# A graph layer on one core: gathers planned with a longer landing and seven tiles kept, first ranks with 128 columns of weights, evictions planned 0.3 later

## The chip, the cores and the metric

The kernel runs on one core of one Trainium2 chip. The metric is the device time of one execution, in microseconds. Before the change the median of three runs is 625.49 us (624.39 to 628.74).

## What is computed

There are 6250 nodes with 128 features each, and 100,000 edges of two types, sorted by their destination. Every edge sends its source's features through the matrix of its type; each node adds up what arrives, adds its own product with a third matrix, and the result goes through a relu, a residual sum and a layer normalisation.

```python
Xs = X[src]
m_data = Xs @ W_data.T + b_data
m_ctrl = Xs @ W_control.T + b_control
msg = jnp.where((edge_types == 0)[:, None], m_data, m_ctrl)
agg = jax.ops.segment_sum(msg, dst, num_segments=X.shape[0])
out = jax.nn.relu(agg + (X @ W_self.T + b_self))
x = _layernorm(x + out)
```

## The kernel before, in words

The nodes are 49 blocks of 128. In the start, `multiply` (L458) forms both products of every block in PSUM (`y`, float32, 128 columns of weights at a time), and `take`, `leave` and `last_part` split each into three bfloat16 parts of 128 columns, together 384: ScalarE copies a part, TensorE subtracts it in PSUM with the matrix `minus` (L483, L496), and so on. The parts stay in SBUF as `m3` and are stored by SP to `table` in DRAM in seven portions of 4, 8, 8, 8, 8, 8 and 5 blocks, two DMAs each (`store`, L509).

35 blocks (`GROUPS`, seven groups of five) sort their edges on the chip. For each group `bucket_hots` (L567) marks edges by source block and type, and `ranks` (L571) gives every edge a place within its bucket: per step of 18, a matmul with `tri` into `acc`, a maximum on VectorE (L584), and a matmul with `rest` into the same `acc`. `fill_a` and `fill_b` (L621, 98 columns, ten matmuls per step `v`) bring the source numbers to their places, ScalarE copies the result (`vs`, L634), and `fill_c` sends it to DRAM (`packed`, L639). `spread` (L739) reads it back, spread over all partitions, as `rows`; `select` (L746) compares it with the partition's number. The main stage then works tile by tile, 25 tiles to a block: `gather` (L775) picks rows of `m3` by matmuls with `rows` as weights into `g_ps` (four banks, `GB`), `evict` (L790) casts them to `gs` (eight tiles, `EB`), mostly on ScalarE, and in the last group partly on VectorE, and `add_up` sums them per destination in `agg` by matmuls with `hot_d`. Nearly all these matmuls have 32 columns of weights and come in fours, one for each strip of the array: `by_columns` (L228, L231) does this.

The other 14 blocks are gathered in another way: `gather_rows` (L877) has GpSimd fetch the rows of 128 edges at a time from `table` by an indirect DMA into `msg` (252 of them, `MB` tiles), once all of `table` is stored, and `gathered_sums` sums them in `agg_g` with `hot_g`. The few edges for which a bucket has no place are fetched on the same GpSimd queue (L715, `mixed`). A finished block goes through `add_parts` (L153), `finish`, `stats`, and by group through `normalise` (L189 on ScalarE) to the output.

The order of instructions on each engine is written by a planner, `Order` (L59). Each part of the work is a stream of steps; a step has a name, a cost for each engine that may take it, names of steps that it needs, and a `lag` between its end on the engine and the time at which others may count on it. The planner holds a time per engine, adds 0.25 between a step and one that needs it, and takes among the steps that could begin next the one that is due first (`due`, L389). Its times only decide the order (and, where two engines may take a step, which one does); on the chip the engines wait for semaphores. A tile's bank or buffer comes free by the same means: gather i needs eviction i - 4, message i needs the gathered sum i - 5.

Of the kernel before, what the change touches and what calls it, by code (L numbers as in the profile page):

```python
# [19 lines left out]
P = 128  # L20
# [7 lines left out]
KT = 18  # L28
# [25 lines left out]
KC = 6  # L54
# [46 lines left out]
def step(name, costs, *needs, lag=0.0):  # L101
    return as_tuple(name), costs, [as_tuple(n) for n in needs], lag


def as_tuple(name):
    return name if isinstance(name, tuple) else (name,)
# [3 lines left out]
def kernel(  # L110
# [94 lines left out]
    with ExitStack() as main:  # L205
        sums_over_windows(main, tc, x, xt, edges, w, bias, table, packed, total,
                          add_parts, finish, load_rows, norm)
# [6 lines left out]
def sums_over_windows(ctx, tc, x, xt, edges, w, bias, table, packed, total,  # L214
                      add_parts, finish, load_rows, norm):
    nc = tc.nc
    V, A, G, T = nc.vector, nc.scalar, nc.gpsimd, nc.tensor
# [7 lines left out]
    order = Order()  # L225
    YB = 4

    def by_columns(out, lhsT, rhs, **flags):  # L228

        for c in range(0, P, 32):  # L230
            T.matmul(out[c : c + 32], lhsT[:, c : c + 32], rhs, **flags)  # L231


    r0 = const.tile([EC, RJ], I32, name="r0")
# [49 lines left out]
    for j in range(RJ):  # L284
# [7 lines left out]
        out=er.rearrange("p k c -> p (k c)"), out_offset=None,  # L292
# [11 lines left out]
    tri = const.tile([P, P], BF16, name="tri")  # L304
    rest = const.tile([P, P], BF16, name="rest")
# [80 lines left out]
    PACE = 1.68  # L386
# [184 lines left out]
    def ranks():  # L571
        for grp, n in enumerate(GROUPS):
            free = [("rank", grp - 1, KT - 1)] if grp else []
            for k in range(KT):
                yield step(("tri", grp, k), {"T": 0.21}, ("hot", grp, k // KC), *free)
                if k == 0:
                    acc = ps_a.tile([P, 512], F32, name="acc")
                    flat = acc[:, : n * NT]
                    by_q = flat.rearrange("p (s q) -> p q s", q=n)
                hot = hots[grp, k // KC][:, k % KC].rearrange("p s q -> p (s q)")  # L580
                by_columns(flat, tri, hot, start=k == 0, stop=False, skip_group_check=True)
                free = []
                yield step(("rank", grp, k), {"V": 0.13 + 0.103 * n}, ("tri", grp, k))
                V.tensor_reduce(slots[grp][:, k, :], by_q, axis=AX.X, op=ALU.max)  # L584
                if k == KT - 1:
                    break
                yield step(("rest", grp, k), {"T": 0.21}, ("rank", grp, k))
                by_columns(flat, rest, hot, start=False, stop=k == KT - 2, skip_group_check=True)

    def fill_a():  # L590
        for grp, n in enumerate(GROUPS):
# [16 lines left out]
    def fill_b():  # L608
        for grp, n in enumerate(GROUPS):
            free = [("listed", grp - 1)] if grp else ["first"]  # L610
            for k in range(KT):
                yield step(("v", grp, k), {"T": 0.07 * n}, ("two", grp, k // KC), *free)
                if k == 0:
                    vts[grp] = ps_a.tile([P, 512], F32, name="small")
                vt = vts[grp][:, : (n + 1) // 2 * NT].rearrange("p (j s) -> p j s", s=NT)
                two = two_s[grp, k // KC]
                hot = hots[grp, k // KC]
                for q in range(n):
                    for i in range(2):
                        c0 = (q % 2 * 2 + i) * R  # L620
                        T.matmul(vt[c0 : c0 + R, q // 2, :], two[:, k % KC, i, :, q],  # L621
                                 hot[:, k % KC, :, q], start=k == 0 and q < 2,
                                 stop=k == KT - 1, skip_group_check=True)
                free = []
# [153 lines left out]
    def evict():  # L778
        for i, (b, g) in enumerate(tiles):
            free = [("s", *tiles[i - EB])] if i >= EB else []  # L780
            if g == NS - 1 and b:
                free.append(("s", b - 1, g))
            costs = {"A": 0.37, "V": 0.53} if b >= STARTS[-1] else {"A": 0.37}
            e = yield step(("e", b, g), costs, ("g", b, g), *free)
            if g < NS - 1:
                gs, at = late.tile([P, D3], BF16, name="gs", bufs=EB), slice(P)
            else:
                gs, at = mixed[blocks[b][0] % 2], slice(2 * R, P)
            gs_tiles[b, g] = gs
            (A.copy if e == "A" else V.tensor_copy)(gs[at], g_tiles.pop((b, g))[at, :D3])  # L790

    def add_up():
        for b, g in tiles:
            grp, q = blocks[b]
            free = [("agg", b)] if g == 0 else [("spilled", grp), ("o", b)] if g == NS - 1 else []
            yield step(("s", b, g), {"T": 0.165}, ("e", b, g), ("d", b, g // DC), *free)
            if g == 0:
                aggs[b] = ps_a.tile([P, D3], F32, name="agg")
            by_columns(aggs[b], d_hots[b, g // DC][:, :, g % DC], gs_tiles.pop((b, g)),
                       start=g == 0, stop=g == NS - 1, skip_group_check=True)  # L800
# [54 lines left out]
    rel_g = const.tile([P, NG, KT], BF16, name="rel_g")  # L855
    msgs, g_hots, kept = {}, {}, []
    GQ = -(-NG // -(-NG // Q))
    MB, XB = 5, 2

    def gathered_fields():  # L860
        yield step("idx", {"V": 1.8}, ("y", NB * 3 // 4), *[("win", b) for b in range(NPB, NB)])
# [10 lines left out]
    def gather_rows():  # L872
        for i, (j, k) in enumerate(gathered):
            free = [("gm", *gathered[i - MB])] if i >= MB else [*stored, "idx"]
            yield step(("msg", j, k), {"G": PACE}, *free, lag=3.0 - PACE)
            msgs[j, k] = late.tile([P, D3], BF16, name="msg", bufs=MB)
            G.indirect_dma_start(  # L877
                out=msgs[j, k], out_offset=None, in_=table[:, :],
                in_offset=bass.IndirectOffsetOnAxis(ap=idx[:, j, k : k + 1], axis=0),
            )  # L880
# [47 lines left out]
    def close_build():  # L928
# [5 lines left out]

    order.run([
        load_x(), starts(), edge_fields(), ranks(), fill_c(), fill_a(), fill_b(),
        spread(), select(), finish_blocks(),
        normalise([(lambda g=g: (hs_[g], mvs[g]), STARTS[g] + q0, q0, n) for g, q0, n in PIECES], "p"), add_up(), gather(), evict(), to_hots(), bucket_hots(),
        multiply(), take(0, "yh", "y"), leave(0, "y1", "yh"),
        take(1, "ym", "y1"), last_part(), constants(), store(), close_build(), add_counts(),  # L940
        finish_gathered(), gathered_sums(), gathered_hots(), gather_rows(), gathered_fields(),
        normalise([(lambda i=i: kept[i], NPB + i * GQ, 0, min(GQ, NG - i * GQ))
                   for i in range(-(-NG // GQ))], "g"),
# [129 lines left out]
```

## Time and profile before

| | |
|---|---|
| median of three runs | 625.49 us |
| the profiled execution's own time | 542.67 us |
| its span, first to last instruction | 540.9 us |
| mean granted TensorE clock | 0.984 |
| TensorE busy, weight loads busy | 507.3 us (94%), 442.9 us (82%) |
| VectorE, ScalarE, GpSimd busy | 432.4, 415.9, 297.4 us |
| L790, ScalarE cast of g_ps to gs | 807, mean 498 ns |
| L775, gather matmuls | 3430, mean 332 ns |
| L231, sums with hot_d, with hot_g | 3360 and 1008, mean 331 and 332 ns |
| L231, ranks with tri and rest | 504 and 476, mean 376 and 378 ns |
| L877, indirect DMAs of msg | 252, mean 1145 ns |

Matmuls on different strips of the array overlap, so the mean of one is not what it adds. SP's work is only issuing and waiting; its rows in a timeline are DMA issues. POOL is GpSimd, ACT ScalarE, DVE VectorE, PE TensorE and PEld its weight loads. A row of a timeline has the start and the duration in microseconds, and in brackets the idle time of the engine before it and what ended it. A row of waits has the total in microseconds, the number of times and the longest.

### The profile page before, as it was taken

To read this page: it belongs to the slowest core of one execution; us is meant where nothing else is said; L and a number is where in the kernel's file an instruction comes from. 1 tells how busy PE (TensorE), PEld (TensorE's weight loads), DVE (VectorE), ACT (ScalarE), POOL (GpSimd) and SP (SyncE) were. 2 spreads that over 40 slices of the span, in tenths; PEclk is the share of its full clock that TensorE was granted. 3 is DMA by queue.
4 is the path that set the end of the run, shared out by engine and by line. 5 is a ranking of instruction groups with operands and counts; after the bars stand their busy time and mean duration, and the time that the engine had idled before them with its cause. 6 is when DMAs were issued, how large, how long until landed. Compare 5 with 4: busy or idle time off the path is not lost.

```text
span 540.9 us, 26355 instructions
## 1 busy us (share of the span) xinstructions
PE 507.3 (94%) x11204; PEld 442.9 (82%) x11204; DVE 432.4 (80%) x967; ACT 415.9 (77%) x1003; POOL 297.4 (55%) x267
## 2 busy tenths in 40 slices
PE   5799977999999999999999999999999999999993
PEld 3546547799887998988989899999998999889882
DVE  5587889578987789978799878999789667668784
ACT  6654356577869788798888888877979879889793
POOL 1000002777687676776567676775757756677500
PEclk9999998799999999999999999999999999999998
DMA  3566875542555425554354542544445454555301
GB/s 94 145 179 191 260 239 193 153 131 79 184 159 161 138 77 179 157 169 134 99 194 139 164 139 81 183 139 160 142 134 162 133 156 135 180 166 164 115 17 35
DMA packets 60932, 79.19 MB, mean 146 GB/s; under 512 B 15760, under 2 KB 51371, under 8 KB 60807
## 3 DMA queue, kind: packets, MB, share of 16 engines
q1 hardware_dynamic: 47253, 49.14, 27.8%
q0 software_dynamic: 12400, 25.08, 16.9%
q10 hardware_dynamic: 1154, 3.21, 1.9%
q8 instruction: 89, 1.46, 1.1%
q14 instruction: 36, 0.29, 0.2%
HBM read 64.35 MB, written 13.05 MB: 143 GB/s over the span
## 4 chain that ended last, share of the span: by engine, by line
PE 73%; DMA 9%; ACT 5%; DVE 5%; issue 3%; SPq 3%; POOL 1%; ACTq 0%; DVEq 0%; POOLq 0%
PE agg L231 25%; PE g_ps L775 23%; PE acc L231 8%; PE agg_g L231 7%; PE small L621 6%; DMA msg<-table,idx 5%; ACT gs L790 2%; DMA rows<-packed 2%; PE y L465 2%; SPq L807 1%; POOL msg L877 1%; ACT h_p L189 1%; SPq L158 1%; DVE slot L584 1%; DVE hot_st L567 1%
## 5 line engine op out<-in xcount | busy, mean ns | idle before, releaser
L790 ACT CAST gs<-g_ps 128x384 bf16<-128x384 f32 x807 | 333.7, 498 | 72.4 <-PE g_ps L775 53.5
L877 POOL DMA_INDIRECT msg<-table,idx x252 | 288.5, 1145 | 115.4 <-PE g_ps L775 46.4
L775 PE MATMUL g_ps<-m,rows 128*32 128x384 bf16 x3430 | 322.4, 332 | 0.9 <-ACT gs L790 0.7
L231 PE MATMUL agg<-gs,hot_d 128*32 128x384 bf16 x3360 | 301.4, 331 | 3.3 <-ACT gs L790 3.3
L231 PEld LDWEIGHTS <-hot_d 128*32 128x32 bf16 x3500 | 195.8, 137 | 13.1 <-issue 7.1
L775 PEld LDWEIGHTS <-rows 128*32 128x32 bf16 x3430 | 189.8, 137 | 18.5 <-issue 12.7
L231 PE MATMUL agg_g<-msg,hot_g 128*32 128x384 bf16 x1008 | 109.1, 332 | 6.2 <-DMA msg<-table,idx 5.8
L584 DVE TENSOR_REDUCE slot<-acc 128x5 bf16<-128x490 f32 x126 | 83.6, 663 | 28.9 <-PE acc L231 17.7
L760 DVE TENSOR_TENSOR hot_d<-count,to 128x1664 bf16<-128x1664 bf16 x70 | 74.4, 1065 | 6.6 <-PE agg L231 6.0
L621 PE MATMUL small<-hot_st,two 128*32 128x98 bf16 x1260 | 70.2, 290 | 0.0
L231 PE MATMUL acc<-hot_st,tri 128*32 128x490 bf16 x504 | 61.8, 376 | 2.1 <-DVE hot_st L567 2.1
L231 PEld LDWEIGHTS <-hot_g 128*32 128x32 bf16 x1008 | 53.5, 123 | 10.6 <-issue 7.8
L231 PE MATMUL acc<-hot_st,rest 128*32 128x490 bf16 x476 | 56.8, 378 | 4.5 <-DVE slot L584 4.0
L621 PEld LDWEIGHTS <-two 128*32 128x32 bf16 x1260 | 58.3, 118 | 2.3 <-DVE two L605 0.6
L715 POOL DMA_INDIRECT mixed<-table,row_i x7 | 6.5, 933 | 92.9 <-DVE hot_g L889 82.3
L476 ACT CAST m<-y 128x512 bf16<-128x512 f32 (+1 forms) x50 | 28.1, 577 | 30.9 <-PE y L483 23.1
L567 DVE TENSOR_TENSOR hot_st<-count,st_b 128x2940 bf16<-128x2940 bf16 x21 | 41.8, 1996 | 7.6 <-PE small L621 5.3
L746 DVE TENSOR_SCALAR rows<-rows,pid 128x3136 bf16<-128x3136 bf16 x35 | 37.0, 1057 | 5.5 <-DMA rows<-packed 5.2
L153 DVE TENSOR_REDUCE whole<-agg 128x128 f32<-128x384 f32 x35 | 19.4, 553 | 17.6 <-PE agg L231 12.8
L465 PE MATMUL y<-w_sb,xt 128*128 128x256 f32 x98 | 33.2, 426 | 0.0
L231 PEld LDWEIGHTS <-rest 128*32 128x32 bf16 x476 | 22.1, 98 | 12.8 <-issue 11.8
L231 PEld LDWEIGHTS <-tri 128*32 128x32 bf16 x504 | 22.4, 99 | 3.3 <-issue 3.1
(144 smaller groups left out, 438.0 us busy)
## 6 DMA issues: line engine op xcount, KB each, us to landing
rows<-packed SPq DMA_DIRECT2D x35, 784.0 KB
table<-m SPq DMA_DIRECT2D x10, 768.0 KB
msg<-table,idx POOLq DMA_INDIRECT x252
xt<-in_xt ACTq DMA_DIRECT2D x5, 512.0 KB
xt_p<-in_xt SPq DMA_DIRECT2D x35, 64.0 KB
xs_p<-in_x SPq DMA_DIRECT2D x35, 64.0 KB
out<-h_p SPq DMA_DIRECT2D x6, 320.0 KB
table<-m SPq DMA_DIRECT2D x2, 480.0 KB
```

The lines of the kernel that those rows point to most:

```text
L153: nc.vector.tensor_reduce(whole, agg.rearrange("p (i c) -> p c i", i=3), axis=AX.X, op=ALU.add)
L231: T.matmul(out[c : c + 32], lhsT[:, c : c + 32], rhs, **flags)
L465: T.matmul(y[:, j, :], xts[g][:, b + j - at_part[g], :], w_sb[:, : 2 * D], start=j == 0, stop=False, skip_group_check=True)
L476: A.copy(part_of(b, n, i), ys[b][:, :n, :].rearrange("p b (t c) -> p t b c", t=2))
L567: V.tensor_tensor(hot, counted[n][:, None, 1 : NT + 1, :].to_broadcast([P, KC, NT, n]), fields[grp][2][:, c * KC : c * KC + KC, None, :].t ...
L584: V.tensor_reduce(slots[grp][:, k, :], by_q, axis=AX.X, op=ALU.max)
L621: T.matmul(vt[c0 : c0 + R, q // 2, :], two[:, k % KC, i, :, q], hot[:, k % KC, :, q], start=k == 0 and q < 2, stop=k == KT - 1, skip_group ...
L746: V.tensor_scalar(rows[b], rows[b], pid1, None, op0=ALU.is_equal)
L760: V.tensor_tensor(hot, counted[DC][:, :, :n], places[grp][:, q, None, c * DC : c * DC + n].to_broadcast([P, P, n]), op=ALU.is_equal)
L775: T.matmul(g_ps[t * R : (t + 1) * R, :D3], rows[b][:, :, s], m3[:, s, :], start=True, stop=True)
L790: (A.copy if e == "A" else V.tensor_copy)(gs[at], g_tiles.pop((b, g))[at, :D3])
L877: G.indirect_dma_start(out=msgs[j, k], out_offset=None, in_=table[:, :], in_offset=bass.IndirectOffsetOnAxis(ap=idx[:, j, k : k + 1], axis=0),
```

## The change

Four things change. `by_columns` gets a width, and the ranks of group 0 use 128: one matmul with 128 columns of weights in place of four with 32. In group 0 the steps `v` are planned six at a time, so that their matmuls follow each other. The lag of an eviction is 0.3 instead of 0. A message is planned with 4.2 instead of 3.0 from its issue to its landing, and seven tiles of `msg` are kept instead of five.

```diff
-    def by_columns(out, lhsT, rhs, **flags):
+    def by_columns(out, lhsT, rhs, width=32, **flags):
 
-        for c in range(0, P, 32):
-            T.matmul(out[c : c + 32], lhsT[:, c : c + 32], rhs, **flags)
+        for c in range(0, P, width):
+            T.matmul(out[c : c + width], lhsT[:, c : c + width], rhs, **flags)
...
     def ranks():
         for grp, n in enumerate(GROUPS):
             free = [("rank", grp - 1, KT - 1)] if grp else []
+            width = 32 if grp else P
...
-                by_columns(flat, tri, hot, start=k == 0, stop=False, skip_group_check=True)
+                by_columns(flat, tri, hot, width, start=k == 0, stop=False, skip_group_check=True)
...
-                by_columns(flat, rest, hot, start=False, stop=k == KT - 2, skip_group_check=True)
+                by_columns(flat, rest, hot, width, start=False, stop=k == KT - 2, skip_group_check=True)
...
-                yield step(("v", grp, k), {"T": 0.07 * n}, ("two", grp, k // KC), *free)
+                if grp:
+                    yield step(("v", grp, k), {"T": 0.07 * n}, ("two", grp, k // KC), *free)
+                elif k % KC == 0:
+                    yield step(("v", grp, k + KC - 1), {"T": 0.07 * n * KC}, ("two", grp, k // KC), *free)
...
-            e = yield step(("e", b, g), costs, ("g", b, g), *free)
+            e = yield step(("e", b, g), costs, ("g", b, g), *free, lag=0.3)
...
-    MB, XB = 5, 2
+    MB, XB = 7, 2
...
-            yield step(("msg", j, k), {"G": PACE}, *free, lag=3.0 - PACE)
+            yield step(("msg", j, k), {"G": PACE}, *free, lag=4.2 - PACE)
```

## The prediction

> **What bounds the kernel now.** I read the page first. TensorE is busy in nearly every slice; the two weak stretches are about 80 to 110 us and the end.
>
> ```profile
> span 540.9 us, 26355 instructions
> PE   5799977999999999999999999999999999999993
> PEclk9999998799999999999999999999999999999998
> ```
>
> The windows view gives the stages: a start up to 80 us, a main stage from 100.5 to 516.5 us and a tail of 16 us after the last gather sum. It also shows the clock at half in 80.1 to 83.5 and 93.7 to 100.5 us (the last three numbers of a line are granted clock, DMA share and GB/s).
>
> ```profile
> 80.10:83.50 3.40, 3.40 (x84) 2.69 (x77) 3.37 (x6) 2.01 (x5) 0.00 (x0) 0.50 1.05 372
> 93.70:100.50 6.80, 5.59 (x76) 3.89 (x79) 0.87 (x5) 1.91 (x4) 5.28 (x6) 0.50 0.43 121
> 100.50:516.50 416.00, 408.35 (x9886) 374.95 (x9882) 346.97 (x755) 346.63 (x860) 287.07 (x252) 1.00 0.47 145
> 516.50:532.50 16.00, 15.62 (x352) 13.31 (x343) 12.18 (x38) 14.78 (x38) 0.00 (x0) 1.00 0.12 33
> ```
>
> Busy time hides small losses, so I counted columns: four strip matmuls of 384 columns start every 0.16 us when nothing stops them. From 100 to 521 us the matmuls hold 371 us of streaming, so 50 us are lost, 15 of them on the tiny matmuls of L621, 15 on gathers (L775), 9 on sums (L231 agg) and 6 on sums of gathered rows. The waits of TensorE after 95 us carry few of these by name:
>
> ```profile
> PE agg_g L231 <- DMA msg<-table,idx: 5.8, 7, 3.5
> PE agg L231 <- ACT gs L790: 3.3, 6, 1.0
> PE g_ps L775 <- ACT gs L790: 0.7, 2, 0.4
> ```
>
> The timeline shows two more. Gathers that follow each other run at the pace of their evictions: sixteen matmuls, four groups, take 1.31 us to the next row instead of 0.65. And in the start a change between 128-wide and 32-wide matmuls costs: the second rank group of 0.20 us is followed by a 128-wide matmul only after 0.32 us.
>
> ```profile
> 101.25 1.54 PE L775 MATMUL g_ps<-m,rows 128*32 128x384 bf16 x16
> 102.56 0.43 PE L231 MATMUL acc<-hot_st,rest 128*32 128x490 bf16 x4
> ...
> 31.18 0.38 PE L231 MATMUL acc<-hot_st,tri 128*32 128x490 bf16 x4
> 31.50 0.39 PE L483 MATMUL y<-m,minus 128*128 128x256 bf16 x2
> 31.72 0.60 PE L465 MATMUL y<-w_sb,xt 128*128 128x256 f32 x2
> ```
>
> What starts the main stage is not TensorE. SP's timeline: the loads end at 69.17, then packed, rows, and the last four table stores.
>
> ```profile
> 68.74 0.43 SPq L158 DMA_DIRECT2D xs_p<-in_x  x1
> 69.27 1.47 SPq L639 DMA_DIRECT2D packed<-vs  x2
> 72.54 1.29 SPq L739 DMA_DIRECT2D rows<-packed  x3
> 73.92 9.75 SPq L509 DMA_DIRECT2D table<-m  x4
> ```
>
> From 73.5 to 88 us these queues move 4.94 MB at 343 GB/s: that is a full DMA system. Rows of block 0 land at 77.84, the first gather starts at 79.92; the stores have landed when GpSimd begins at 90.36; its first message reaches TensorE at 94.9, after 3.50 us of idling.
>
> **What the Trainium skill says.** "TensorEngine Tiling (Array Packing)", Key Properties: changing the tiling mode drains the array. The trace agrees, at about 0.1 us a change (0.32 against 0.20 above; 0.2 from L467 at 30.76 to the ranks at 30.96, of which 0.107 is streaming). "TensorE: Matmul & The Clock Gate", Part 1: after an idle window of some 3.4 us the clock halves. The trace agrees: 3.4 and 6.8 us at 0.50. "DMA: Bandwidth & Descriptors", Queues, rings and completion order: descriptors of one row are consumed in ring order. The trace agrees: the stores behind rows took 4.02 us to issue, against 0.4 to 0.6 for earlier ones.
>
> **The change, part by part.** Sums are against the profiled execution's 542.7 us (span 540.9 and 1.8 around it). The median of the runs, 625.5, is 82.8 above; no view shows these, and I carry them over unchanged.
>
> *128-wide ranks, and six steps of v in one piece.* The 18 tri and 17 rest steps of group 0 become 35 matmuls instead of 140. Streaming is the same: 490 columns in four strips at once or in one piece are 0.204 us. Weights of 128 columns take 0.10 us (L467, L483), covered by the matmul before; 128-wide pairs of 256 columns already follow each other at 0.22 us with new weights. If that cover is gone, 35 x 0.1 = 3.5 us come back. Counted in the built order, changes of width before the last L483/L496 fall from 49 to 17: 32 x 0.1 = 3.2 us of TensorE time less. The 180 tiny matmuls are the same ones, in three blocks of 60.
>
> *What this moves on SP.* The built order puts the table stores of part 5 (2 x 768 KB) ahead of packed and rows; before they stood behind. Part 5's y now ends about 4 us earlier on TensorE (1.75 us less in front of block 43's y, and 30 changes of width), so the stores are ready near 69 us, when SP reaches them. But 1.57 MB at 343 GB/s is 4.6 us in the same rings, in front of packed. Packed lands near 76 instead of 72.5, rows 5.3 us later near 81.4, the selection (1.04) and a semaphore make the first gather about 82.7: 2.8 late. I compare by time minus the streaming done so far, since all streaming has to be done: at the first gather 79.92 - 46.79 = 33.1 now, 82.7 - 46.38 = 36.3 then. After it come 60 tiny matmuls (2.3 us where their columns need 0.6: 1.7), half clock until about 87 us (2) and small pauses (1): 41.0. The first gather sum stands after 53.3 us of streaming, so TensorE gets there at 94.3; only 0.96 MB of stores are left behind rows, all stores land 1 to 2 us earlier, and the first message is there near 93.3: no stall, and no second half-clock stretch. Now the message comes at 94.9, after 55.6 us of streaming: 39.3, and 5.6 us at half clock cost 2.8 more: 42.1. Net -1 us; bounds -4 (packed not held up) and +4 (part 5 late).
>
> *Landing planned at 4.2, seven tiles.* Each gather sum now stands farther behind the sum that frees its buffer: median 10.3 us of matmul work instead of 7.3, the least 5.5 instead of 4.1. The chain shows landings of 4.0 to 6.4 us. So of the six waits after the first (5.8 - 3.5 = 2.3 us) I take -2; bounds 0 and -2.3. GpSimd issues the same 252 gathers at 1.25 us apiece; more buffers also cover its waits for L715's index.
>
> *Evictions planned 0.3 later.* No instruction is added. The lag also delays, in the plan, the gather that reuses the bank. A gather needs 0.33 + 0.49 and about 0.08 of semaphores, 0.9 us, after the gather four before it. In the built order 47 of them stand closer than that, short by 8.5 us together; in the changed one 22, by 3.6. A delay pushes its followers too, so not all is paid: -3, bounds 0 and -5. From gather to sum the distance hardly moves (median 1.52 to 1.48 us), and ScalarE still has its runs of four or five scalings (L189, eight both times): the 3.3 us of waits for gs stay, 0 (-1 to +1).
>
> *The tail.* After the last gather sum the changed order has 18.8 us of matmul work, not 14.2, and 55 evictions, of which ScalarE has 46 and VectorE 9 (before 42: 28 and 14). ScalarE's pace is 0.38: 46 x 0.38 + nine scalings x 0.39 + three roots x 0.25 = 21.7 us, so ScalarE, not TensorE, sets it. Loss by position: 21.7 - 18.8 = 2.9, and some 1 us of waits, against 16.0 - 14.2 = 1.8 now: +2, bounds 0 and +4.
>
> Sum: -1 - 2 - 3 + 0 + 2 = -4 us: 538.7 profiled, 621.5 as a median (-0.6%).
>
> **Rivals.** *Faster by more:* the pauses between gathers go in full (-5), messages never wait (-2.3), packed isn't held and both half-clock stretches shrink (-4), tail +0.5: -11, 614.5. For it: each loss is in the trace. Against it: the DMA queues are full just there. *Slower, by part 5's stores:* they stand first on SP, and packed waits for them in program order. If block 43's copies come as late as now (stores issued at 73.92, not 69.27), packed lands near 81, rows 86, the first gather at 87.7: 41.3 where it was 33.1, and with the same 1.7, 2 and 1 us 46.0 against 42.1: +4. With the tail at +4 and only 1 us of message waits saved, +7: 632.5. It decides from about 71 us for those copies. For it: ScalarE and VectorE pass that chain, and VectorE is over 80% busy there. *The change does little:* waits removed in the main stage come back as others: within 1 us of 625.5; it lies in the likeliest case's range.
>
> **How the numbers follow.** Within 1% (6.3 us, about what a measurement of this kernel can tell from no change) with a likeliest 621.5 and own range 617 to 629: 0.5. The faster case 0.3, the slower 0.2. Leaving out a tenth on each side gives 613 to 633. Faster by over 1%: 0.32, with a share of the first case; slower 0.19; between 0.49.
>
> **What would show it.** Right: changes of width gone from 25 to 70 us, packed issued after a pair of stores and landing near 76, first gather at 82 to 83, no half clock after 95, no gather sum waiting for a message, fewer runs of bare gathers at 0.38, and ScalarE without a gap in the last 22 us. Wrong: first gather before 79 or after 85 us, messages that still wait, or a new wait on VectorE's ranks in the main stage, which a new order can bring and no count here excludes.

## The result, and the profile after

The changed kernel takes 646.2 us as a median of four runs (643.1 to 648.5) against 624.9 beside it: a ratio of 1.0332, 95% interval 1.0276 to 1.0388. I had forecast 621.5, in a range of 613 to 633. The kernel before takes 541 to 548 us in some groups of runs and 622 to 640 in others, so each run is compared with runs of the kernel before made beside it, and "at 545" and "at 630" name the two kinds of group.

The page of the changed kernel shows TensorE in the same two weak places, and a thin spread of eights and sevens in the main stage.

```profile
span 644.9 us, 26150 instructions
PE   6899578897989998898898989989998899888895
PEclk9899887999899999999999999999999999899999
```

The windows view (duration, then busy time and instructions of TensorE, weight loads, VectorE, ScalarE, GpSimd, then granted clock, DMA share, GB/s) gives the main stage up to the last gather sum, as in the prediction, and the tail after it.

```profile
100.50:613.80 513.30, 458.42 (x9808) 373.97 (x9812) 346.72 (x761) 350.11 (x856) 276.56 (x251) 0.98 0.40 118
613.80:637.10 23.30, 23.04 (x481) 17.66 (x470) 12.50 (x38) 22.00 (x58) 0.00 (x0) 1.00 0.06 16
```

The main stage is what grew: before, 9886 matmuls took 416 us; here 9808 take 513. It did not grow by work: VectorE and ScalarE are busy for about as long as before (347 and 350 us; before 347 and 347), and the DMA rate is lower (118 GB/s against 145). The waits of TensorE say what else is there.

```profile
PE agg L231 <- issue: 13.3, 38, 0.9
PE g_ps L779 <- issue: 13.1, 28, 1.1
PE agg L231 <- ACT gs L794: 11.5, 23, 1.0
PE g_ps L779 <- ACT gs L794: 5.0, 10, 1.7
```

The first two lines are waits for nothing that the profile knows: TensorE's next matmul had all it needed and did not start. The page of before has no such line for these matmuls. By the prediction's own count (columns streamed against time) the main stage lost 50 us before and loses 149 now, from 100 us to GpSimd's last gather.

SP's timeline shows the start as the built order had said: stores of part 5, then packed, then rows.

```profile
68.15 1.00 SPq L509 DMA_DIRECT2D table<-m  x2
69.25 2.58 SPq L643 DMA_DIRECT2D packed<-vs  x2
75.97 1.30 SPq L743 DMA_DIRECT2D rows<-packed  x3
```

These two pages can't be compared as they stand. The page of before was taken at 545 (542.7 us in a kernel whose timed runs took 625), that of after at 630. The experiments therefore start with that. No profile of the kernel before itself was taken at 630; the kernel with the 128-wide ranks alone, further down, stands in for it.

### The profile page after: what moved, and what is told of

The parts are those of the page before. It is cut to its first block, busy times and chain, and to the rows that moved or that the text cites. A ratio compares the mean times of both kernels' runs of the same rounds, so it can differ in the third digit from the quotient of the medians.

```text
span 644.9 us, 26150 instructions
## 1 busy us (share of the span) xinstructions
PE 560.4 (87%) x11099; PEld 444.3 (69%) x11099; DVE 428.5 (66%) x960; ACT 423.2 (66%) x1010; POOL 288.4 (45%) x267
## 4 chain that ended last, share of the span: by engine, by line
PE 76%; issue 6%; DVE 6%; ACT 5%; DMA 4%; SPq 1%; POOL 0%; another core or an unknown queue 0%; ACTq 0%; DVEq 0%; POOLq 0%
PE agg L231 28%; PE g_ps L779 25%; PE acc L231 8%; PE agg_g L231 7%; PE small L625 6%; ACT gs L794 3%; DMA table<-m 2%; DVE slot L585 1%; DVE hot_st L567 1%; PE y L465 1%; DMA packed<-vs 1%; ACT h_p L189 1%; DMA msg<-table,idx 1%; DVE m L493 1%; ACT m L476 1%
## 5 line engine op out<-in xcount | busy, mean ns | idle before, releaser
L794 ACT CAST gs<-g_ps 128x384 bf16<-128x384 f32 x814 | 341.0, 496 | 169.8 <-PE g_ps L779 98.4
L881 POOL DMA_INDIRECT msg<-table,idx x252 | 278.4, 1105 | 216.2 <-PE agg_g L231 96.4
L779 PE MATMUL g_ps<-m,rows 128*32 128x384 bf16 x3430 | 343.1, 339 | 23.5 <-issue 13.1
L231 PE MATMUL agg<-gs,hot_d 128*32 128x384 bf16 x3360 | 316.3, 341 | 24.2 <-ACT gs L794 11.5
L231 PEld LDWEIGHTS <-hot_d 128*32 128x32 bf16 x3500 | 204.4, 137 | 69.6 <-issue 57.1
L779 PEld LDWEIGHTS <-rows 128*32 128x32 bf16 x3430 | 193.6, 139 | 52.8 <-issue 40.8
L231 PE MATMUL acc<-hot_st,tri 128*32 128x490 bf16 (+1 forms) x450 | 62.1, 385 | 2.7 <-DVE hot_st L567 2.2
L231 PE MATMUL acc<-hot_st,rest 128*32 128x490 bf16 (+1 forms) x425 | 57.0, 381 | 7.0 <-DVE slot L585 4.5
L465 PE MATMUL y<-w_sb,xt 128*128 128x256 f32 x98 | 31.7, 411 | 0.0
L231 PEld LDWEIGHTS <-rest 128*32 128x32 bf16 (+1 forms) x425 | 21.6, 100 | 13.6 <-issue 11.1
L231 PEld LDWEIGHTS <-tri 128*32 128x32 bf16 (+1 forms) x450 | 21.7, 101 | 5.9 <-issue 5.2
```

The costliest lines, as they stand in the source:

```text
L231: T.matmul(out[c : c + width], lhsT[:, c : c + width], rhs, **flags)
L465: T.matmul(y[:, j, :], xts[g][:, b + j - at_part[g], :], w_sb[:, : 2 * D], start=j == 0, stop=False, skip_group_check=True)
L779: T.matmul(g_ps[t * R : (t + 1) * R, :D3], rows[b][:, :, s], m3[:, s, :], start=True, stop=True)
L881: G.indirect_dma_start(out=msgs[j, k], out_offset=None, in_=table[:, :], in_offset=bass.IndirectOffsetOnAxis(ap=idx[:, j, k : k + 1], axis=0),
```

## The experiments

**Which execution does the page of before show?** The unchanged kernel, and each part of the change alone. Theory 1 was that the page is of an execution unlike the timed ones; its rival, that the 83 us lie outside the span.

> The kernel before, unchanged. Theory 1 (the page that the prediction read is of an execution unlike the timed ones): its span is about 623 us, 83 us more than the 540.9 of that page, and the losses lie along the whole main stage as waits named issue and as later starts of evictions, as in the changed kernel's trace. Rival (the 83 us lie outside the span): the span is about 541 us again and the time 625.

Measured: 543.98 us, 0.9993 [0.9973, 1.0012], a span of 542.3, and no wait for "issue" of the kind above. Neither theory came: the timed runs were fast as well. So before has a whole group of runs at 544, not one odd execution.

The ranks and the blocks of six `v`, without the rest:

```diff
+            width = 32 if grp else P
...
+                by_columns(flat, tri, hot, width, start=k == 0, stop=False, skip_group_check=True)
...
+                elif k % KC == 0:
+                    yield step(("v", grp, k + KC - 1), {"T": 0.07 * n * KC}, ("two", grp, k // KC), *free)
```

> Only the ranks of group 0 with 128 columns and the steps v in sixes. Theory 1 (the loss of 21 us is of the main stage, from the lag of evictions or the gathers): within 4 us of before. Rival A (packed behind part 5's stores delays the start): 5 to 20 us slower than before.

Measured, at 545: 547.29 us, 1.0074 [1.0034, 1.0115], some 4 us. Its waits:

```profile
PE g_ps L779 <- DVE rows L750: 4.6, 1, 4.6
PE agg_g L231 <- DMA msg<-table,idx: 4.9, 5, 3.0
```

The first gather waits 4.6 us for its rows (they are late behind part 5's stores, as predicted; it starts at 82.25), and the first gather sum still waits 3.0 us for its message, which I had said would be gone. Up to 100 us TensorE loses 18.1 us against 14.6. The saving itself did come: from 25 us to the last subtraction (L483, L496) TensorE loses 1.4 us where it lost 3.8, and the wait for the rows swallows it.

The messages alone:

```diff
-    MB, XB = 5, 2
+    MB, XB = 7, 2
...
-            yield step(("msg", j, k), {"G": PACE}, *free, lag=3.0 - PACE)
+            yield step(("msg", j, k), {"G": PACE}, *free, lag=4.2 - PACE)
```

> Only the gathers: landing planned at 4.2 and seven tiles. Theory 1 in its form B (seven tiles let GpSimd issue gathers in bursts, beside which the other engines run late): 10 to 20 us slower than before. If the loss is of the evictions' lag: within 4 us of before, or a few us faster.

Measured, at 545: 541.47 us, 0.9944 [0.9926, 0.9962]: -3 us, near the -2 of the prediction, and not the +10 to +20 of theory 1 (bursts of gathers), which comes back below. One wait for a message is left where there were seven.

```profile
PE agg_g L231 <- DMA msg<-table,idx: 4.0, 1, 4.0
```

The evictions alone:

```diff
-            e = yield step(("e", b, g), costs, ("g", b, g), *free)
+            e = yield step(("e", b, g), costs, ("g", b, g), *free, lag=0.3)
```

> Only the evictions planned 0.3 later. Theory 1 in its form A (the lag puts the blocks behind the gathered sums and leaves a tail set by ScalarE): 10 to 20 us slower than before. If the loss is of the gathers or of the start: within 4 us of before.

Measured, at 545: 546.88 us, 1.0057 [1.0031, 1.0083]: +3 us where I had summed -3 and +2 for the tail.

```profile
PE agg_g L231 <- DMA msg<-table,idx: 15.1, 12, 4.1
```

The loss on gathers did fall, in the count of columns from 15 us to 9. But with the kernel's own 3.0 us for a landing, the new order asks for messages sooner: 12 waits and 15.1 us where there were 7 and 5.8. The stall that was removed came back as another.

So at 545 the parts give +0.74, -0.56 and +0.57%, together +0.75%, and nothing like 3.3%. Either they don't add, or the 3.3% belongs to runs at 630. The next four ran together, at 630: the whole change again, the change without the evictions, the change without the ranks, and the 128-wide ranks alone with `v` one by one as before (SP's order then stays that of before).

> The whole change. Theory 2 (the parts add up: ranks +0.74%, gathers -0.56%, evictions +0.57%, and the 3.3% belongs to the condition in which both kernels took 80 to 100 us more): 0.5 to 1.0% slower than before, 547 to 550 us. Rival (the parts do not add: the three orders together make something that none makes alone): 2.5 to 4% slower, 558 to 566 us.

> The change without the lag of evictions (ranks and gathers). Theory 2: +0.2%, about 545.5 us. Rival: as slow as the whole change if ranks with gathers make it, else under 1%.

> The change without the 128-wide ranks and the v steps in sixes (gathers and evictions). Theory 2: within 0.3% of before, and no gather sum waits for its message, since seven tiles stand against the later evictions. Rival: as slow as the whole change if gathers with evictions make it.

> Only the 128-wide ranks of group 0, with the steps v one by one as before. If the ranks' loss of 0.74% is made by the order on SP (part 5's stores ahead of packed), which this kernel has only if its order has it too: as before or up to 3 us faster where packed stands ahead, 3 us slower where it does not. If the loss is of the blocks of sixty tiny matmuls: as before or faster.

Measured: 653.57 us, 1.0314 [1.0276, 1.0352]; 653.08, 1.0292 [1.0252, 1.0332]; 655.02, 1.0319 [1.0262, 1.0376]; and 634.25, 0.9993 [0.9965, 1.0022]. The first three share only the edits on the messages, which were a gain at 545. The width alone costs and saves nothing in the time that can be measured. It takes out only 20 of the changes of width before the last subtraction (49 to 29, where the ranks with `v` in sixes reach 17), since the 32-wide matmuls of `v` still stand between the ranks.

The last kernel has nearly the order of before, and so shows where 90 us go at 630. Its first gather of a message is at 90.3 us (before at 545: 91.5), and 31.7 us follow its last one (before: 31.3). All of the difference lies between them, while GpSimd gathers: of the 95 us between the two spans, 93 are streaming time that TensorE loses there (142.9 against 49.7, counted as before). Its timeline of TensorE there:

```profile
236.57 0.37 PE L231 MATMUL agg_g<-msg,hot_g 128*32 128x384 bf16 x2
237.30 0.39 PE L231 MATMUL agg_g<-msg,hot_g 128*32 128x384 bf16 x2 [0.36 <-issue]
237.34 0.39 PE L776 MATMUL g_ps<-m,rows 128*32 128x384 bf16 x2
238.06 0.38 PE L776 MATMUL g_ps<-m,rows 128*32 128x384 bf16 x2 [0.33 <-issue]
```

A group of four strips is broken in the middle: two start, and the next two, which wait for nothing, start 0.7 us later. At 545 the traces of before hold no such pause after 100 us (over 0.3 us from one start to the next, no semaphore to wait for); this one holds 45.

**Which edit of the two?** Seven tiles and 4.2 us apart, both together again, and the whole change with the tiles cut back to five. With seven tiles alone every engine's instruction order is that of before; with 4.2 alone it is that of both together; in the fourth it is that of the whole change.

```diff
-    MB, XB = 5, 2
+    MB, XB = 7, 2
```

> Seven message tiles alone, the planned 3.0 us kept, so that every engine gets its instructions in the order of the kernel before and only waits on message tiles differ. Where the kernel before takes about 625 to 635 us: theory A (more gathered rows outstanding at once disturb TensorE's supply) expects +2 to +3.3%, theory B (the order planned with 4.2 us disturbs it) expects 0 within 0.5%. Where the kernel before takes about 544 us both expect 0 to -0.4% (message waits shorter).

```diff
-            yield step(("msg", j, k), {"G": PACE}, *free, lag=3.0 - PACE)
+            yield step(("msg", j, k), {"G": PACE}, *free, lag=4.2 - PACE)
```

> Planned with 4.2 us alone, five message tiles kept. Its order on every engine is that of the kernel with both edits. Where the kernel before takes about 625 to 635 us: theory A expects 0 to +1%, theory B +2 to +3.3%, with the lost time in TensorE waits that the waits view puts down to issue. Where the kernel before takes about 544 us: -0.2 to -0.6%.

> Both edits on the messages (4.2 us and seven tiles), as in an earlier run, which gave -0.56% where the kernel before took 544 us. Where it takes about 625 to 635 us both theories expect +2.5 to +3.3%; a third (the parts only cost together with the ranks or the evictions) expects 0 within 0.6%. Where it takes about 544 us: -0.4 to -0.7% again.

The fourth, against the changed kernel:

```diff
-            msgs[j, k] = late.tile([P, D3], BF16, name="msg", bufs=MB)
+            msgs[j, k] = late.tile([P, D3], BF16, name="msg", bufs=5)
```

> The whole change with the tiles of the messages cut back from seven to five at the last moment, the planner still counting on seven: the order on every engine is that of the changed kernel. Where the kernel before takes about 625 to 635 us: theory A 0 to +1%, theory B +2.5 to +3.5%. Where it takes about 544 us: +0.2 to +1.2%, the cost of the ranks and the evictions less the gain of the messages.

Measured, at 630: seven tiles 652.23 us, 1.0411 [1.0356, 1.0466]; 4.2 us 630.60, 1.0055 [1.0011, 1.0098]; both 647.46, 1.0344 [1.0295, 1.0393]; the whole change with five tiles 639.51, 1.0233 [1.0174, 1.0291]. The order is not the cause: with it unchanged, two more tiles cost 4.1%. Theory B falls. Theory A holds for the edits on the messages, but not cleanly for the whole: there the tiles account for about one point of 3.3, and it had put the rest at 0 to 1%. At 630 the parts don't add.

What do tiles do? They let GpSimd run ahead. In the kernel with seven tiles, GpSimd's timeline holds this, five gathers in a row at its fastest pace,

```profile
240.20 0.95 POOL L877 DMA_INDIRECT msg<-table,idx  x1 [0.30 <-issue]
241.45 0.95 POOL L877 DMA_INDIRECT msg<-table,idx  x1 [0.30 <-issue]
242.70 0.94 POOL L877 DMA_INDIRECT msg<-table,idx  x1 [0.30 <-PE g_ps L775]
243.95 0.95 POOL L877 DMA_INDIRECT msg<-table,idx  x1 [0.30 <-issue]
245.20 1.00 POOL L877 DMA_INDIRECT msg<-table,idx  x1 [0.30 <-issue]
```

and TensorE's holds this beside it:

```profile
239.97 0.55 PE L775 MATMUL g_ps<-m,rows 128*32 128x384 bf16 x4 [0.22 <-ACT gs L790]
241.48 0.39 PE L775 MATMUL g_ps<-m,rows 128*32 128x384 bf16 x4 [0.95 <-issue]
243.70 0.55 PE L775 MATMUL g_ps<-m,rows 128*32 128x384 bf16 x4 [1.83 <-ACT gs L790]
247.94 0.55 PE L775 MATMUL g_ps<-m,rows 128*32 128x384 bf16 x4 [3.70 <-ACT gs L790]
```

The pauses grow with the row: 0.95, 1.83, 3.70 us. The last two are put down to ScalarE's casts, but ScalarE was idle too: the cast before 247.94 starts 3.2 us after the end shown for the matmuls that it reads. "Perfetto Trace Analysis" of the Trainium skill, Summary: the profiler window per engine type, says that TensorE's end in a trace is an estimate. That fits a matmul that ended late inside TensorE; a late signal would look the same, and no run here tells them apart. Over the whole trace, casts that waited for TensorE start 0.10 us (median) after the matmuls' end shown when no gather was issued in the last 1.5 us, 0.15 behind one and 0.42 behind two in a row (39, 114 and 18 casts); from ScalarE to TensorE it is 0.05 us in all three cases. At 545, in the traces of before and of both edits, the first numbers stay between 0.10 and 0.12. The windows view of twelve such microseconds in two kernels shows how much it is. With seven tiles, at 630, seven gathers:

```profile
239.00:251.00 12.00, 5.30 (x68) 3.12 (x64) 4.44 (x12) 3.54 (x8) 6.62 (x7) 0.66 0.37 112
```

With seven tiles and 4.2, at 545, nine gathers:

```profile
240.00:252.00 12.00, 12.00 (x303) 11.47 (x298) 10.05 (x23) 9.23 (x24) 8.61 (x9) 1.00 0.48 155
```

68 matmuls against 303, and a granted clock of 0.66 on top. I then counted, over nine traces at 630 and five at 545, TensorE's pauses over 0.3 us without a wait (start to start, as above), each put down to the last gather issued in the 3 us before it, by the time since the gather before that one:

| since the gather before | gathers at 630 | pauses each | gathers at 545 | pauses each |
|---|---|---|---|---|
| under 1.3 us | 407 | 0.72 | 479 | 0.01 |
| 1.3 to 1.6 | 88 | 0.48 | 282 | 0.00 |
| 1.6 to 1.7 | 274 | 0.24 | 120 | 0.00 |
| 1.7 to 1.8 | 375 | 0.09 | 51 | 0.00 |
| 1.8 to 3.5 | 982 | 0.06 | 298 | 0.00 |

So a new theory S: at 630 TensorE falters beside gathers that GpSimd issues close together, and more tiles let it issue them so. Rival N: it is the number of gathered rows outstanding, or where the tiles lie. A filler on GpSimd behind each gather keeps the tiles and takes the closeness away:

```diff
+    pause = const.tile([P, 384], F32, name="pause")
...
                 in_offset=bass.IndirectOffsetOnAxis(ap=idx[:, j, k : k + 1], axis=0),
             )
+            G.iota(pause, pattern=[[1, 384]], base=0, channel_multiplier=0,
+                   allow_small_or_imprecise_dtypes=True)
```

> The kernel before (five tiles, 3.0 us) with a filler on GpSimd behind each gather of message rows, so that two gathers start at least 1.75 us apart instead of 1.25. Where the kernel before takes about 625 to 635 us: theory S (gathers issued close together make TensorE pause) expects the pauses without a wait to fall from some 45 to under 20 and the time to fall by 1.5 to 3%; theory N (the number of gathered rows outstanding, or the place of the tiles) expects 0 to +0.5%. Where the kernel before takes about 544 us: 252 gathers at 1.75 us are 441 us, with 90 us ahead and 32 us behind them 563 us, so +3%.

The same with 192 elements, the same (384) in the whole change, and, without a filler, four tiles in place of five (`bufs=4`):

> As before it with half the filler: gathers at least 1.55 us apart, where the traces show 0.4 pauses a gather in place of 0.7. Where the kernel before takes about 625 to 635 us: theory S expects -0.5 to -1.5%, between no filler and the longer one; theory N 0. Where it takes about 544 us: 0 to +0.5%, since 252 x 1.55 us do not bind.

> The whole change, seven tiles and all, with the longer filler behind each gather. Where the kernel before takes about 625 to 635 us: theory S expects the +3.3% gone, -2.5 to +0.5% against the kernel before, although as many tiles are outstanding; theory N expects +3 to +3.5%. Where it takes about 544 us: +3%, bound by the gathers.

> Four message tiles in place of five, the planner not told, so that the order on every engine is that of the kernel before. Where the kernel before takes about 625 to 635 us: theory N (number outstanding) expects -1 to -3%; theory S expects what the runs of close gathers give: fewer of them, and more waits on messages, -1 to +0.5%. Where it takes about 544 us: +0.5 to +2%, waits on messages alone.

Measured, at 630: the filler in the kernel before 623.04 us, 0.9794 [0.9716, 0.9872]; half of it 631.23, 0.9946 [0.9923, 0.9969]; in the whole change 632.03, 0.9945 [0.9924, 0.9966]; four tiles 631.26, 0.9968 [0.9944, 0.9991]. In the groups of GpSimd's instructions of the first:

```profile
L878 POOL DMA_INDIRECT msg<-table,idx x252 | 281.6, 1117 | 76.1 <-PE g_ps L775 34.0 <-PE agg_g L231 26.1 <-issue 8.4
L882 POOL IOTA pause<- 128x384 f32 x252 | 127.1, 504 | 2.2
```

127 us of work that does nothing were added to GpSimd, and the kernel became 2.1% faster. (The 0.3 us of gap behind a gather shrink behind the filler, so the closest gathers are 1.59 us apart, not the 1.75 that I had written; with half the filler 1.43, not 1.55.) The whole change, with its seven tiles, goes from +3.3 to -0.5%. Rival N falls as the main cause; the dose has the right sign. The number of gathers on their way can be read too, a gather counted as landed when the last of its 16 packets of 4608 bytes ends: three or more are on their way (itself counted) at 33 of 252 issues with five tiles (width alone), at 31 with seven and at 37 with the filler. So neither the tiles nor the filler changed that number much, and it does not carry the effect. Against the filled kernel before, the whole change is still some 1.5% slower, about what its ranks and evictions cost at 545 (1.3%).

One thing that S expected did not happen: in the kernel before the pauses without a wait did not become fewer, 51 with the filler against 45 (width alone); in the whole change they fell from 65 and 70 to 45. The table above says why. Without the filler 35 gathers stand under 1.3 us behind the one before and 2 at 1.3 to 1.6; with it none and 69. At the table's rates that makes some 44 pauses without the filler and 50 with it: the filler is too short to leave the spacings at which TensorE pauses. What fell are the long stalls. Time lost by TensorE beyond streaming, from 100 us to the last gather, one trace each, in us, with the time at half clock and the runs of three or more gathers that stand under 1.3 us behind each other:

| kernel, at 630 | lost | in stalls over 1 us | in stalls of 0.3 to 1 us | at half clock | runs of close gathers |
|---|---|---|---|---|---|
| width alone (order as before) | 142.9 | 21.0 | 58.7 | 23.9 | 2 |
| 4.2 alone | 137.8 | 21.1 | 56.1 | 10.2 | 3 |
| four tiles | 137.1 | 18.8 | 60.7 | 3.4 | 2 |
| seven tiles | 159.4 | 36.6 | 59.0 | 43.9 | 8 |
| seven tiles and 4.2 | 154.0 | 31.6 | 57.0 | 35.3 | 10 |
| whole change, and again | 148.6, 154.1 | 22.1, 23.9 | 66.3, 72.0 | 20.5, 17.1 | 7, 7 |
| whole change less evictions | 161.6 | 31.5 | 57.3 | 44.4 | 9 |
| whole change less ranks | 158.7 | 28.7 | 61.8 | 36.6 | 9 |
| whole change with five tiles | 144.1 | 16.3 | 66.5 | 17.1 | 7 |
| filler 384 in before | 130.0 | 10.5 | 58.8 | 4.3 | 0 |
| filler 192 in before | 138.2 | 22.2 | 58.8 | 11.2 | 0 |
| filler 384 in whole change | 135.7 | 16.6 | 54.6 | 3.4 | 0 |
| before, at 545 | 49.7 | 1.3 | 8.1 | 0.5 | 22 |

With seven tiles the close gathers come in 7 to 10 runs, with four or five in 2 or 3, and with a filler in none. The exception is the whole change with five tiles, whose order alone makes 7; this fits that taking the tiles back gave back so little there. At 545 there are 22 runs, and yet hardly any long stall.

The granted clock is part of the price. In the trace with seven tiles TensorE is busy for 1.20 of 3.40 us at full clock, and then has half of it for 10.2 us:

```profile
239.50:242.90 3.40, 1.20 (x10) 0.49 (x10) 0.74 (x3) 0.90 (x2) 2.49 (x4) 1.00 0.57 185
242.90:253.10 10.20, 5.71 (x73) 3.79 (x76) 3.28 (x7) 3.43 (x8) 3.64 (x4) 0.50 0.20 55
```

The timed runs agree: their median clock is 0.956 with seven tiles against 0.982 in the kernel before, and 0.985 with the filler against 0.978. By an estimate from these (clock withheld times span), the clock accounts for at most 17 of the 26 us that seven tiles cost, and for at most 5 of the 12 us that the filler saves. It is not what makes TensorE pause: 42 of the 45 pauses of the width-alone kernel begin at full clock.

Two last runs asked whether the short pauses go too when gathers stand 1.8 us apart: the filler with 832 elements, in the kernel before and with the two edits on the messages.

> The kernel before with a filler of some 0.77 us on GpSimd behind each gather, so that gathers start at least 1.8 us apart. Where the kernel before takes about 625 to 635 us: theory S expects the stalls over 1 us and the short pauses both to fall, and -3 to -5%; if only the long stalls depend on the spacing, -1.5 to -2.5%, as with 1.55 us; GpSimd alone would allow 90 + 252 x 1.82 + 32 = 581 us. Where it takes about 544 us: +6 to +7% (581 us), bound by the gathers.

> The same filler with seven tiles and the 4.2 us. Where the kernel before takes about 625 to 635 us: theory S expects the same as the run with five tiles within 1% (the two edits gave +3.4% without the filler); if the number outstanding costs by itself, +2 to +3% over it. Where it takes about 544 us: +6 to +7%.

Measured, both at 545 this time: 668.3 us, 1.2229 [1.2176, 1.2281], and 673.3, 1.2316 [1.2253, 1.2378]. TensorE's waits, and GpSimd's groups, of the first:

```profile
PE agg_g L231 <- DMA msg<-table,idx: 98.1, 85, 3.8
```

```profile
L878 POOL DMA_INDIRECT msg<-table,idx x252 | 287.6, 1141 | 43.0 <-issue 19.3 <-PE g_ps L775 16.9 <-PE agg_g L231 2.9
L882 POOL IOTA pause<- 128x832 f32 x252 | 212.7, 844 | 1.9
```

There GpSimd is the bound: 287.6 + 212.7 + 43.0 + 1.9 + 8.2 for the gathers of L715 are 553 us from 91.8 on, which ends at 645 (the last gather stands at 643.3), and some 28 us follow. I had foreseen the bound but put it at 581 us, with the shortest gather (0.95 us) and a filler of 0.77 in place of their means, 1.14 and 0.84. The question itself is left unanswered: at 630 this spacing wasn't measured, and neither was the short filler at 545. Seven tiles give no gain here since nothing runs ahead.

## Why the prediction was wrong

**The step that failed** is the first of the sum: "The median of the runs, 625.5, is 82.8 above; no view shows these, and I carry them over unchanged." These 82.8 us are no constant around the kernel. They are TensorE's falterings while GpSimd gathers, between 90 and 605 us (93 us lost more in the trace with nearly the order of before, of 95 between the spans), and the edits on the messages make them longer: +3.4% at 630 where they gave -0.56% at 545. The page that I reasoned from holds none. A page 83 us under the median was itself the sign that it couldn't answer for the median, and there the fault was mine rather than the trace's.

**Landing at 4.2, seven tiles.** The mechanism named was right and its size nearly, at 545: -3.0 us against -2, six waits of seven gone. "GpSimd issues the same 252 gathers at 1.25 us apiece" took the shortest spacing for all of them: the median is 1.5 us at 545 (before) and 1.8 at 630 (width alone), and it says nothing of how often the shortest ones follow each other. At 630 the tiles alone cost +4.1%.

**128-wide ranks and SP.** The saving on TensorE was right: with ranks and sixes the changes of width before the last L483/L496 fall from 49 to 17, and TensorE loses 2.5 us less from 25 us to there, where 3.2 were summed. The order on SP went as worked out (packed behind part 5's stores, first gather at 81.5 in the changed kernel, 82.25 with the ranks alone, 82.7 predicted). The issue of 4.02 us that was read as ring order does not show it, since with the ranks alone the stores behind rows take 0.61 and 0.69 us; that packed waits behind stores shows in its landing, 4.1 us from the end of its issue to the issue of rows, against 1.8 before. What failed is "all stores land 1 to 2 us earlier, and the first message is there near 93.3: no stall": with the ranks alone GpSimd begins at 91.2 (before 91.5), the message is summed at 94.8 (94.9 in the changed kernel), and the second half-clock stretch stayed. Net +4 us in place of -1.

**Evictions.** "Runs of gathers at 0.38 fewer" was right (loss on gathers 15 to 9 us); that nothing takes its place was wrong: +9 us of waits for messages. Net +3.1 with its tail, in place of -3 and +2.

**Tail.** Right. From the last gather sum to the last matmul 23.3 us, of which 18.8 were counted as matmul work: a loss of 4.5 against 2.1 before (16.3 less 14.2), so +2.4 where +2 was put; ScalarE is busy 22.0 of 23.3.

By its own terms, at 545, the sum would have been +4 us and not -4; the other 16 to 17 us of the 21 measured are left for what only the runs at 630 have. The rival "slower, by part 5's stores" named the right place for the smaller share, but its premise did not come (block 43's copies late, first gather at 87.7), and it stops 14 us short of what was measured.

What stays open: why TensorE falters beside gathers in some groups of runs and not in others (the record numbers the chip of the experiments' groups: 5 at 545, then 10, 6 and 1 at 630, then 1 again at 545, so that number alone does not decide it), by what path (the instruction queue in the page carries 88 or 89 packets of 16 KB in both, with a median of 0.97 us with seven tiles and 0.99 in before; it is 1.13 and 0.96 in the two traces of the changed kernel, so slower fetches don't explain it), whether the closeness of gathers alone does it (a filler also shifts each gather against TensorE's work, and no run shifts them without spacing them), and how the cost of the whole change divides at 630, where undoing the tiles gives back one point of 3.3 and spacing the gathers gives back all. Whether the whole change gains or loses at 545 was only added up from its parts.

## What to carry to other kernels

When the page's execution and the timed runs differ by more than a few per cent, find out first what the page lacks; a difference may not be carried over as a constant, because the change may act on it. More buffers for a gather on GpSimd remove waits, but they also let the gathers bunch, so look at the spacing of their issues and not only at their number. Short stalls of TensorE can also cost clock, so compare the granted clock of the timed runs. A small filler that spaces the gathers can pay (-2.1% here at 630; at 545 it was not measured), but count its floor with mean durations: a filler of 0.84 us made GpSimd the bound and cost 22% at 545.

## What was not expected of the hardware

TensorE can pause in the middle of a group with nothing to wait for: 44 to 72 times in each trace at 630, mostly 0.3 to 0.7 us at a time and 1.5 at most; 0 to 3 times in the traces at 545. At 630, behind two gathers under 1.3 us apart there are 0.72 such pauses, behind two that are 1.8 to 3.5 us apart 0.06. Beside such gathers ScalarE starts later after the end shown for TensorE's matmuls (0.10 us without a gather near, 0.42 behind two in a row, 3.2 once), but TensorE does not start later after ScalarE (0.05). After 3.4 us in which it was busy for 1.2, its clock was half for 10.2 us. A change between 128-wide and 32-wide matmuls costs about 0.08 us (2.5 us for 32). Of 94 us between two executions of nearly one program, none lies before the first gather or after the last.
